# Layer 3's softmax denominators in a four-layer graph network: inverted on 128 nodes at a time instead of once for each feature

## The chip, the cores and the metric

The kernel runs on one core of one Trainium2 chip. The metric is the device time of one execution in microseconds (us); lower is better. The engines are named as in the profile: PE (TensorE), PEld (its weight loads), DVE (VectorE), ACT (ScalarE), POOL (GpSimd) and SP (the queue that issues most DMAs).

## What is computed

Sixteen graphs of 1024 nodes with 128 features pass through four layers. Each layer is a graph layer on the 0/1 matrix adj, a residual and a layer norm. Layer 0 is attention with one head, layer 1 attention with eight heads and an ELU, layer 2 a mean over neighbours with weights, and layer 3, which the change is in, is attention with four heads of 32 features:

```python
def _L3_gnn_ref(features, adj_matrix, W):
    D = W.shape[-1]                                        # 32
    Wh = jnp.einsum('bsf,hfd->bhsd', features, W)          # 4 heads
    scores = jnp.einsum('bhsd,bhtd->bhst', Wh, Wh) / jnp.sqrt(jnp.float32(D))
    scores = jnp.where(adj_matrix[:, None, :, :] > 0, scores, NEG_INF)
    attn = jax.nn.softmax(scores, axis=-1)
    h = jnp.einsum('bhst,bhtd->bhsd', attn, Wh)
    return jnp.transpose(h, (0, 2, 1, 3)).reshape(B, S, H * D)
...
x = _layernorm(x + _L3_gnn_ref(x, adj, L3_gnn_W), axis=-1)
```

The kernel divides by the softmax's denominator (the sum of the exponentials) after the sum over neighbours, once for each node and head.

## The kernel before, in words

Everything below is in `tile_binary`, the function that runs when adj holds only 0 and 1. The second function, `tile_general`, is in the program too, but this input doesn't run it.

**The order of the work.** The functions `before0`, `layer0`, `before1`, `layer1`, `last1`, `layer2`, `before3` and `layer3` issue nothing themselves. They record steps, each with an engine, an assumed duration, a due time and the buffers that it reads and writes. `Plan.run` then walks through all steps once, when the program is built, and writes out a fixed order for every engine: on each engine, of the steps that could start first, it takes the one with the earliest due time. So graph b's layer 1, graph b+1's layer 0 and graph b-1's layer 3 stand interleaved. Due times come from the last lines of the function: graph b is due at b * PERIOD, and each part of it at an offset from that. Some constants shape the order: URGENT makes ACT and DVE steps earlier that touch PSUM, AHEAD limits how far beyond the earliest open due time a step may be taken, LATER1 and LATER3 put off the weighted sums of layers 1 and 3 behind their weights. On the chip each engine keeps its order and waits for its inputs by semaphores. The assumed durations take no part in that.

**Buffers.** Pools have few places. "wk" in PSUM has two of 1024 numbers a partition, and takes all short products; "acc1" and "acc3" have two of 512 each, for layer 1's and layer 3's accumulators. In SBUF, "z" (9 places) holds layer 1's weights, "z3" (5 places) layer 3's, "oT1" (one place, 1024 wide) layer 1's result before it is transposed and the exponentials of its ELU, "oT3" (one place, 512 wide) layer 3's, and "rest" (one place) a piece of layer 2's and layer 3's inverted sums.

**Layer 1** is most of DVE's work: L778 makes each weight tile of 128x1024 in one instruction, and L786 multiplies it into acc1. At the end of a group of heads ACT copies acc1 into oT1 (L816), PE transposes it (L366), and DVE inverts the sums that lie in the transposed tile (L831) and multiplies (L835).

**Layer 2** runs its 192 products a graph in one burst (L918). Ahead of it L886 and L893 on DVE take products out of "wk".

**Layer 3** works on one half of the nodes (512) at a time, with 8 blocks of 128 neighbours in each. For a block, ACT makes the mask (L1066), PE adds the mask (L1076) and the scores (L1086) into two "wk" places, ACT takes exponentials (L1129), and PE adds the weighted features into one acc3 place, "values" (L1098), and the sums of weights into the other, "sums" (L1108). In some blocks DVE first adds the weights of two blocks (L1143), so that their sum is taken once. Both accumulators have features on the partitions, four heads of 32, and the 512 nodes along the free axis. The sums therefore stand there 32 times for each head, one for each feature. At the end of a half DVE inverts all 128x512 sums (L1156) into "rest", multiplies the values by them into "oT3" (L1159), PE transposes the result into "wk" (L366, the helper `transposes`), and DVE adds it to x3 (L1170) and takes row sums (L405) for the layer norm, which runs on ACT (L430, L458), DVE and POOL (L446).

Of the kernel before, what the change touches and what calls it, by code (L numbers as in the profile page):

```python
# [24 lines left out]
ALU = mybir.AluOpType  # L25
# [3 lines left out]
P = 128  # L29
HALF = 512  # L30
# [46 lines left out]
class Plan:  # L77
# [4 lines left out]

    LAG = 0.2
    SLACK = 0.00
    URGENT = 67.5
    SWITCH = 0.1
    SAME = 0.0
    AHEAD = 346.0

    def __init__(self):  # L90
        self.steps = []
# [13 lines left out]
    def step(self, engine, us, due, emit, reads=(), writes=(), lag=None, holds=(), floor=0.0, mode="full"):  # L105
        s = Step(engine, us, due, emit, self.LAG if lag is None else lag, mode)
        s.ready = floor
        for buf in holds:
            s.bufs.append(buf)
            buf.left += 1  # L110
        follows = set()
        for keys, writing in ((reads, False), (writes, True)):
            for key in keys:
                buf, part = key if isinstance(key, tuple) else (key, None)
                if buf not in s.bufs:
                    s.bufs.append(buf)
                    buf.left += 1
                buf.parts.setdefault(part, [None, []])
                for p, (writer, readers) in buf.parts.items():
                    if part is None or p is None or p == part:  # L120
                        if writer:
                            follows.add(writer)
                        if writing:
                            follows.update(readers)
        for keys, writing in ((reads, False), (writes, True)):
            for key in keys:
                buf, part = key if isinstance(key, tuple) else (key, None)
                if writing:
                    for p in list(buf.parts):
                        if part is None or p == part:  # L130
                            buf.parts[p] = [s, []]
                else:
                    buf.parts[part][1].append(s)
        follows.discard(s)
        if engine in ("ACT", "DVE") and any(buf.pool in self.scarce for buf in s.bufs):
            s.due -= self.URGENT
        s.waits = len(follows)
        for f in follows:
            f.next.append(s)
        self.steps.append(s)  # L140
        return s
# [83 lines left out]
def tile_binary(  # L225
# [20 lines left out]
    nc = tc.nc  # L246
    B, N, F = x.shape
    NB = N // P
    HB = NB // 2
    H1, _, D1 = w1.shape  # L250
    H3, _, D3 = w3.shape
# [17 lines left out]
    ident = const.tile([P, P], F32, name="b_ident")  # L269
# [20 lines left out]

    TOGETHER = {(0, 3), (1, 3)}
    LATER1 = 7.4
    LATER3 = 15.9


    sbuf = ctx.enter_context(tc.tile_pool(name="bsbuf", bufs=1))
# [2 lines left out]
    def places(pool, count, shape, dtype=F32):  # L299
        tiles = [sbuf.tile(shape, dtype, name=f"{pool}_{n}") for n in range(count)]  # L300
        plan.pool(pool, tiles)
        return tiles

    def little(pool, shape):
        if pool not in plan.places:
            places(pool, 2, shape)
        return Buf(pool, pool)
# [29 lines left out]
    places("xT0", 2, [P, HALF])  # L337
    places("rest", 1, [P, HB, P])
    places("rT", 1, [H1 * NB, P])
    places("whT", 3, [P, HALF])  # L340
    places("turn", 3, [P, HALF])
    places("gap", 6, [P, HALF], BF16)
# [11 lines left out]
    step = plan.step  # L354
# [5 lines left out]
    def blocks_of(t):  # L360

        return t.rearrange("p (k c) -> p k c", c=P)

    def transposes(pt, parts):
        for k, part in enumerate(parts):
            nc.tensor.transpose(pt[:, k * P : (k + 1) * P], part, ident)  # L366
# [42 lines left out]
    def layernorm(y, tot, due, rest=None, half=None):  # L409


        off, squared, rstd, shift = (little(n, [P, NB]) for n in ("off", "squared", "rstd", "shift"))
        junk = little("junk", [P, P])
        ks = slice(0, NB) if half is None else slice(half * HB, (half + 1) * HB)
        pairs = range(ks.start // 2, ks.stop // 2)
        tot_of = (tot, half)

        def minus_mean():
            if rest:
                nc.vector.scalar_tensor_tensor(  # L420
                    off.t, in0=tot.t, scalar=-1.0 / F, in1=rest.t, op0=ALU.mult, op1=ALU.add
                )
            else:
                nc.vector.tensor_scalar(off.t[:, ks], tot.t[:, ks], -1.0 / F, None, ALU.mult)  # L424

        step("DVE", 0.1, due, minus_mean, [tot_of, rest] if rest else [tot_of], [off])

        def square(pair):
            for k in (2 * pair, 2 * pair + 1):
                nc.scalar.activation(  # L430
                    junk.t, y.t[:, k, :], AF.Square, bias=off.t[:, k : k + 1], accum_out=squared.t[:, k : k + 1]
                )

        for pair in pairs:
            step(
                "ACT", 1.05, due + pair, lambda pair=pair: square(pair), [off, (y, pair // 2)], [(squared, pair), junk]
            )
        due += 4
        step(
            "DVE", 0.1, due,  # L440
            lambda: nc.vector.tensor_scalar(rstd.t[:, ks], squared.t[:, ks], 1.0 / F, EPS, ALU.mult, ALU.add),  # L441
            [squared], [rstd],
        )
        step(
            "POOL", 2.3, due,
            lambda: nc.gpsimd.tensor_tensor(rstd.t[:, ks], rstd.t[:, ks], neg_half[:, ks], ALU.pow),  # L446
            [], [rstd], lag=0.3,
        )
        due += 3
        step(  # L450
            "DVE", 0.1, due,
            lambda: nc.vector.tensor_tensor(shift.t[:, ks], off.t[:, ks], rstd.t[:, ks], ALU.mult),  # L452
            [off, rstd], [shift],
        )

        def apply(pair):
            for k in (2 * pair, 2 * pair + 1):
                nc.scalar.activation(  # L458
                    y.t[:, k, :], y.t[:, k, :], AF.Identity, bias=shift.t[:, k : k + 1], scale=rstd.t[:, k : k + 1]
                )  # L460

        for pair in pairs:
            step("ACT", 0.77, due + pair, lambda pair=pair: apply(pair), [shift, rstd], [(y, pair // 2)])
# [380 lines left out]
    def last1(b, due):  # L844

        G = graphs[b]
        o, x1, e = G["x2"], G["x1"], Buf("oT1", "e")
        step(
            "ACT", 1.0, due, lambda: nc.scalar.activation(e.t, o.t.rearrange("p k f -> p (k f)"), AF.Exp), [o], [e]
        )  # L850
        step(
            "DVE", 1.14, due,
            lambda: nc.vector.scalar_tensor_tensor(o.t, in0=o.t, scalar=0.0, in1=x1.t, op0=ALU.max, op1=ALU.add),
            [x1], [o],
        )
        step(
            "DVE", 1.14, due,
            lambda: nc.vector.scalar_tensor_tensor(o.t, in0=blocks(e.t), scalar=1.0, in1=o.t, op0=ALU.min, op1=ALU.add),
            [e], [o],
        )  # L860
        tot = little("tot", [P, NB])
        for half in range(2):
            sums(o, half, tot, due)
        layernorm(o, tot, due + 3)
# [185 lines left out]
    def layer3(b, due, span):  # L1050
# [1 line left out]
        x3, m, whTs, turns, low, hhs = G["x3"], G["m"], G["whT"], G["turn"], G["low"], G["hh3"]  # L1052
        tot = little("tot", [P, NB])

        def flat(rest):
            return rest.t.rearrange("p k c -> p (k c)")

        for half in range(2):
            cols = slice(half * HALF, (half + 1) * HALF)

# [55 lines left out]
            for j in range(NB):  # L1116
# [33 lines left out]
                else:  # L1150
# [1 line left out]
                        "PE", 0.87, at + LATER3, lambda j=j, zs=zs, f=summed: f(j, zs), zs, [sums3], mode="32 columns"  # L1152
                    )
            at = due + span * (half + 1) / 2
            oT, pt, rest = Buf("oT3", "oT3"), Buf("wk", "pb3"), Buf("rest", "shares")
            step("DVE", 0.6, at, lambda sums3=sums3, rest=rest: nc.vector.reciprocal(flat(rest), sums3.t), [sums3], [rest])  # L1156
            step(
                "DVE", 0.6, at,
                lambda values=values, rest=rest, oT=oT: nc.vector.tensor_tensor(oT.t, values.t, flat(rest), ALU.mult),  # L1159
                [values, rest], [oT],  # L1160
            )
            step(
                "PE", 0.44, at,
                lambda oT=oT, pt=pt: transposes(pt.t, [oT.t[:, k * P : (k + 1) * P] for k in range(HB)]),
                [oT], [pt],
            )
            ks = slice(half * HB, (half + 1) * HB)
            step(
                "DVE", 0.6, at,
                lambda ks=ks, pt=pt: nc.vector.tensor_tensor(  # L1170
                    x3.t[:, ks, :], x3.t[:, ks, :], blocks_of(pt.t[:, :HALF]), ALU.add
                ),
                [pt], [(x3, half)],
            )
            sums(x3, half, tot, at)
            if b == B - 1:
# [12 lines left out]


    PERIOD = 131.4
    weights(-213)
    for b in range(B):
        at = b * PERIOD
        at0 = 71 if b == 1 else at
        before0(b, at0 - 52)
        layer0(b, at0)
        before1(b, at - 70)
        layer1(b, at + 82, 123)
        last1(b, at + 184)  # L1200
        layer2(b, at + 147)
        before3(b, at + 175)
        layer3(b, at + 302, 133)
    with tc.manual_schedule():
        plan.run()
# [626 lines left out]
```

## Time and profile before

| what | value |
|---|---|
| median of three runs | 2421.48 us (2417.6 to 2427.45) |
| the profiled execution's own time | 2421.31 us |
| its span in the profile | 2419.5 us |
| mean granted PE clock | 0.961 |
| busy: PE, DVE, ACT, POOL | 2122.6, 2037.9, 1684.1, 284.4 us |
| layer 3's reciprocal, L1156 | 32 instructions, 107.2 us busy, 3351 ns each |
| layer 3's multiply L1159, and add L1170 | 32 each, 692 and 681 ns each |
| first and last L1156 | 318.2 and 2401.0 us |

How to read the profile: a row names the line, the engine, the operation, the tiles written and read, the shapes and the number of instructions; then come the busy time in us and the mean duration of one in ns, then the idle time of the engine just before these instructions and what ended it. The chain of waits is followed back from the last instruction: at each step to the work that released it, or to the instruction before it on the same engine. A stretch row gives, for a stretch of time, the busy time of each engine in it. fp32 products are two records each in the profile, since PE runs them in two passes.

### The profile page before, as it was taken

The numbers are of one execution on the slowest core, as the hardware profiler recorded it, in microseconds if no ns is written. First come the engines' busy times: TensorE is split into PE (matmuls) and PEld (weight loads), VectorE is DVE, ScalarE is ACT, GpSimd is POOL, SyncE is SP. The second block draws the span as 40 slices with busy tenths as digits, with TensorE's granted clock in tenths as the row PEclk, the third lists the DMA queues.
The fourth block names the chain that finished last, engine by engine and source line by source line (L and its number), as shares of the span: only waits on it lengthen the run. The fifth ranks groups of instructions, "written<-read, shape, count | busy, mean of one in ns | idle before, by whom it ended". The sixth has DMA issues, their size and how long they took to land.

```text
span 2419.5 us, 50524 instructions
## 1 busy us (share of the span) xinstructions
PE 2122.6 (88%) x21040; PEld 991.1 (41%) x21040; DVE 2037.9 (84%) x2659; ACT 1684.1 (70%) x4150; POOL 284.4 (12%) x268
## 2 busy tenths in 40 slices
PE   5758799899999999999999989999999989898876
PEld 5416244353535344353544435353534426242321
DVE  3899789889989898999989898999999979898322
ACT  3314667678586868868686977868686876767684
POOL 2000011101011011101111110101101110100000
PEclk8879899999999999999999999999999999999998
DMA  6211220403122040312204041222204131200000
GB/s 101 68 54 28 82 34 19 88 28 89 28 88 37 10 98 27 91 26 89 36 31 93 11 95 30 85 31 89 36 10 97 27 82 25 71 10 10 1 10 11
DMA packets 80832, 119.55 MB, mean 49 GB/s; under 512 B 7384, under 2 KB 58704, under 8 KB 80592
## 3 DMA queue, kind: packets, MB, share of 16 engines
q1 hardware_dynamic: 62160, 99.43, 12.1%
q0 software_dynamic: 18432, 16.79, 8.5%
q8 instruction: 167, 2.74, 0.5%
q14 instruction: 73, 0.60, 0.1%
HBM read 157.55 MB, written 8.97 MB: 69 GB/s over the span
## 4 chain that ended last, share of the span: by engine, by line
DVE 39%; PE 36%; ACT 17%; issue 5%; DMA 2%; POOL 2%; POOLq 0%; DVEq 0%; ACTq 0%
DVE z L778 24%; PE wk L918 7%; PE acc L786 6%; PE acc L638 6%; ACT z L1129 5%; PE wk L1086 4%; PE acc L1098 4%; DVE rest L1156 4%; PE wk L366 3%; ACT junk L430 3%; PE acc L1108 3%; ACT turn L1003 2%; ACT x L458 2%; DVE z L1143 2%; PE wk L1076 2%
## 5 line engine op out<-in xcount | busy, mean ns | idle before, releaser
L778 DVE SCALAR_TENSOR_TENSOR z<-R,q,m 128x1024 f32<-128x1024 f32 x1024 | 1253.7, 1278 | 18.9 <-PE acc L786 10.2
L1129 ACT ACTIVATE z<-wk,low 128x1024 f32<-128x1024 f32 x512 | 545.6, 1107 | 88.3 <-PE wk L1086 79.6
L786 PE MATMUL acc<-z,hh 128*32 128x512 f32 x4096 | 526.0, 628 | 80.0 <-DVE z L778 75.0
L430 ACT ACTIVATE junk<-x,off 128x128 f32<-128x128 f32 x640 | 257.4, 402 | 317.3 <-DVE off L424 293.6
L446 POOL TENSOR_TENSOR rstd<-rstd,b_neg_half 128x8 f32<-128x8 f32 (+1 forms) x81 | 176.8, 2183 | 1196.9 <-DVE rstd L441 1056.6
L1086 PE MATMUL wk<-whT,turn 32*128 32x512 f32 x2048 | 297.9, 652 | 0.0
L458 ACT ACTIVATE x<-x,shift,rstd 128x128 f32<-128x128 f32 x640 | 261.6, 490 | 46.3 <-DVE shift L452 46.2
L1098 PE MATMUL acc<-z,hh 128*32 128x512 f32 x2048 | 280.0, 616 | 14.1 <-DVE rest L1156 14.1
L1108 PE MATMUL acc<-z,ones 128*32 128x512 f32 x1792 | 261.1, 614 | 28.7 <-DVE z L1143 27.8
L786 PEld LDWEIGHTS acc<-z,hh 128*32 128x32 f32 x4096 | 115.1, 113 | 390.7 <-issue 209.1
L638 PEld LDWEIGHTS acc<-hd,z 128*128 128x128 f32 x2048 | 240.2, 194 | 59.5 <-ACT x L659 19.0
L638 PE MATMUL acc<-hd,z 128*128 128x129 f32 x2048 | 252.9, 280 | 10.4 <-ACT x L659 8.9
L918 PEld LDWEIGHTS <-m 128*128 128x128 fp8e5 x3072 | 179.0, 98 | 16.5 <-issue 16.5
L918 PE MATMUL wk<-y,m 128*128 128x128 bf16 (+1 forms) x3072 | 180.7, 219 | 3.5 <-ACT z L1129 3.5
L1066 ACT ACTIVATE gap<-m,neg_one 128x512 bf16<-128x512 fp8e5 x256 | 183.3, 720 | 0.0
L1076 PE MATMUL wk<-gap,far 32*32 32x512 bf16 x4096 | 133.9, 389 | 50.4 <-ACT z L1129 19.1
L626 DVE SCALAR_TENSOR_TENSOR z<-R,q,m 128x512 f32<-128x512 f32 x240 | 165.1, 745 | 8.9 <-DMA R<-rows 8.9
L1076 PEld LDWEIGHTS <-far 32*32 32x32 bf16 x4096 | 43.0, 88 | 265.2 <-issue 262.9
L1156 DVE RECIPROCAL rest<-acc 128x512 f32<-128x512 f32 x32 | 107.2, 3351 | 39.0 <-PE acc L1108 39.0
L1108 PEld LDWEIGHTS acc<-z,ones 128*32 128x32 f32 x1792 | 50.1, 110 | 184.5 <-issue 120.2
L430 ACT ACTIVATION_READ_ACCUMULATOR junk<-x,off 128x1 f32 x640 | 120.4, 188 | 0.0
L1098 PEld LDWEIGHTS acc<-z,hh 128*32 128x32 f32 x2048 | 48.8, 110 | 150.0 <-issue 123.6
(115 smaller groups left out, 1914.1 us busy)
## 6 DMA issues: line engine op xcount, KB each, us to landing
R<-rows SPq DMA_DIRECT2D x139, 512.0 KB
m<-in_adj_dram POOLq DMA_DIRECT2D x128, 128.0 KB, 4.7
xT<-in_xT_dram SPq DMA_DIRECT2D x32, 256.0 KB
x<-in_x_dram SPq DMA_DIRECT2D x16, 512.0 KB
out_dram<-x SPq DMA_DIRECT2D x15, 512.0 KB
rows<-rT SPq DMA_DIRECT2D x16, 32.0 KB
out_dram<-x SPq DMA_DIRECT2D x2, 256.0 KB
z<-in_L_gnn_a_dram SPq DMA_DIRECT2D x2, 128.0 KB
```

What stands on the lines that cost most here:

```text
L430: nc.scalar.activation(junk.t, y.t[:, k, :], AF.Square, bias=off.t[:, k : k + 1], accum_out=squared.t[:, k : k + 1])
L458: nc.scalar.activation(y.t[:, k, :], y.t[:, k, :], AF.Identity, bias=shift.t[:, k : k + 1], scale=rstd.t[:, k : k + 1])
L638: nc.tensor.matmul(av[k // 2].t.rearrange("p (k c) -> p k c", k=2)[:, k % 2, : P + 1], lhsT=z.t[:, at : at + P], rhs=hd.t[:, j, : P + 1], ...
L778: nc.vector.scalar_tensor_tensor(z.t, in0=G["R"][h].t, scalar=q.t[:, j, h : h + 1], in1=m[j].t, op0=ALU.max, op1=ALU.mult)
L786: nc.tensor.matmul(av[half].t[32 * c : 32 * c + 32, :], lhsT=hh.t[:, j, at : at + 32], rhs=zs[c].t[:, half * HALF : (half + 1) * HALF], st ...
L918: nc.tensor.matmul(ps.t[:, k * SLOT : k * SLOT + part.stop - part.start], lhsT=m[j].t[:, rows_i], rhs=y2.t[:, j, part], start=j == 0 and n ...
L1076: nc.tensor.matmul(sc[h // 2].t[c * 32 : (c + 1) * 32, (h % 2) * HALF : (h % 2 + 1) * HALF], lhsT=far[rows_r, rows_r], rhs=gap.t[rows_r, : ...
L1086: nc.tensor.matmul(sc[h // 2].t[:, (h % 2) * HALF : (h % 2 + 1) * HALF], lhsT=turns[j // HB].t[rows_h, j % HB * P : (j % HB + 1) * P], rhs ...
L1098: nc.tensor.matmul(values.t[rows_h, :], lhsT=hhs[j // HB].t[:, j % HB, rows_h], rhs=zs[h // 2].t[:, h % 2, :], start=j == 0, stop=j == NB - 1,
L1108: nc.tensor.matmul(sums3.t[h * D3 : (h + 1) * D3, :], lhsT=ones, rhs=zs[h // 2].t[:, h % 2, :], start=j == 0, stop=j == NB - 1,)
L1129: lambda g=g, sc=sc, zs=zs: nc.scalar.activation(zs[g].t.rearrange("p h n -> p (h n)"), sc[g].t, AF.Exp, bias=low.t, scale=S3),
L1156: step("DVE", 0.6, at, lambda sums3=sums3, rest=rest: nc.vector.reciprocal(flat(rest), sums3.t), [sums3], [rest])
```

## The change

In layer 3 the values and the sums are now both copied out of PSUM by ACT, into the two halves of one "oT1" place. PE then brings both to a layout with nodes on the partitions: the values by the four transposes as before, and the sums by four products with every 32nd column of the identity, which picks one number of each head. A group of 128 nodes thus gives four columns, and a half gives 16 a partition. DVE inverts these 16, multiplies the transposed values by them with a broadcast over the 32 features, into "rest", and adds the result to x3. "oT3" is left to the squares in `before3`. The layer norm's "junk" has one place in place of two. The planner's constants and the due offsets of most parts have other values.

```diff
-    URGENT = 67.5
+    URGENT = 79.2
...
-    AHEAD = 346.0
+    AHEAD = 411.0
...
-    LATER3 = 15.9
+    LATER3 = 20.9
...
+    places("junk", 1, [P, P])
...
-        junk = little("junk", [P, P])
+        junk = Buf("junk", "junk")
...
-            oT, pt, rest = Buf("oT3", "oT3"), Buf("wk", "pb3"), Buf("rest", "shares")
-            step("DVE", 0.6, at, lambda sums3=sums3, rest=rest: nc.vector.reciprocal(flat(rest), sums3.t), [sums3], [rest])
+            oT, pt, o = Buf("oT1", "oT3"), Buf("wk", "pb3"), Buf("rest", "o3")
+            rd = little("rd3", [P, HB, H3, 1])
+            for n, of in enumerate((values, sums3)):
+                step(
+                    "ACT", 0.48, at,
+                    lambda n=n, of=of, oT=oT: nc.scalar.copy(oT.t[:, n * HALF : (n + 1) * HALF], of.t), [of], [(oT, n)],
+                )
+
+            def natural3(oT=oT, pt=pt):
+
+                for k in range(HB):
+                    at, at0 = HALF + k * H3, HALF + k * P
+                    nc.tensor.matmul(
+                        pt.t[:, at : at + H3], lhsT=oT.t[:, at0 : at0 + P], rhs=ident[:, 0:P:D3],
+                        start=True, stop=True,
+                    )
+                transposes(pt.t, [oT.t[:, k * P : (k + 1) * P] for k in range(HB)])
+
+            step("PE", 0.8, at, natural3, [oT], [pt])
+
+            def share(pt=pt, rd=rd, o=o):
+                nc.vector.reciprocal(
+                    rd.t, pt.t[:, HALF : HALF + HB * H3].rearrange("p (k h u) -> p k h u", k=HB, u=1)
+                )
+                nc.vector.tensor_tensor(
+                    o.t.rearrange("p k (h d) -> p k h d", h=H3),
+                    pt.t[:, :HALF].rearrange("p (k h d) -> p k h d", k=HB, h=H3),
+                    rd.t.to_broadcast([P, HB, H3, D3]),
+                    ALU.mult,
+                )
+
+            step("DVE", 0.8, at, share, [pt], [rd, o])
+            ks = slice(half * HB, (half + 1) * HB)
             step(
                 "DVE", 0.6, at,
-                lambda values=values, rest=rest, oT=oT: nc.vector.tensor_tensor(oT.t, values.t, flat(rest), ALU.mult),
-                [values, rest], [oT],
-            )
-            step(
-                "PE", 0.44, at,
-                lambda oT=oT, pt=pt: transposes(pt.t, [oT.t[:, k * P : (k + 1) * P] for k in range(HB)]),
-                [oT], [pt],
-            )
...
-                lambda ks=ks, pt=pt: nc.vector.tensor_tensor(
-                    x3.t[:, ks, :], x3.t[:, ks, :], blocks_of(pt.t[:, :HALF]), ALU.add
-                ),
-                [pt], [(x3, half)],
+                lambda ks=ks, o=o: nc.vector.tensor_tensor(x3.t[:, ks, :], x3.t[:, ks, :], o.t, ALU.add),
+                [o], [(x3, half)],
             )
...
-    weights(-213)
+    weights(-196)
...
-        before0(b, at0 - 52)
+        before0(b, at0 - 45)
...
-        before1(b, at - 70)
-        layer1(b, at + 82, 123)
-        last1(b, at + 184)
-        layer2(b, at + 147)
-        before3(b, at + 175)
+        before1(b, at - 66)
+        layer1(b, at + 82, 124)
+        last1(b, at + 146)
+        layer2(b, at + 129)
+        before3(b, at + 198)
```

More of the change, by code (lines that the diff above doesn't have):

```diff
@@ L1053, in layer3 @@
         tot = little("tot", [P, NB])
-        def flat(rest):
-            return rest.t.rearrange("p k c -> p (k c)")
         for half in range(2):
@@ L1154, in layer3 @@
             at = due + span * (half + 1) / 2
-            oT, pt, rest = Buf("oT3", "oT3"), Buf("wk", "pb3"), Buf("rest", "shares")
-            step("DVE", 0.6, at, lambda sums3=sums3, rest=rest: nc.vector.reciprocal(flat(rest), sums3.t), [sums3], [rest])
-            step(
-                "DVE", 0.6, at,
-                lambda values=values, rest=rest, oT=oT: nc.vector.tensor_tensor(oT.t, values.t, flat(rest), ALU.mult),
-                [values, rest], [oT],
-            )
-            step(
-                "PE", 0.44, at,
-                lambda oT=oT, pt=pt: transposes(pt.t, [oT.t[:, k * P : (k + 1) * P] for k in range(HB)]),
-                [oT], [pt],
-            )
+            oT, pt, o = Buf("oT1", "oT3"), Buf("wk", "pb3"), Buf("rest", "o3")
[25 more added lines that the diff above has]
+            step("DVE", 0.8, at, share, [pt], [rd, o])
             ks = slice(half * HB, (half + 1) * HB)
```

## The prediction

> **What bounds the kernel now.** I read first the page's busy shares, then the chain of waits, then the busy time by stretch for the steady part, and last what TensorE waits for there.
>
> ```profile
> PE 2122.6 (88%) x21040; PEld 991.1 (41%) x21040; DVE 2037.9 (84%) x2659; ACT 1684.1 (70%) x4150; POOL 284.4 (12%) x268
> DVE 39%; PE 36%; ACT 17%; issue 5%; DMA 2%; POOL 2%; POOLq 0%; DVEq 0%; ACTq 0%
> DVE z L778 24%; PE wk L918 7%; PE acc L786 6%; PE acc L638 6%; ACT z L1129 5%; PE wk L1086 4%; PE acc L1098 4%; DVE rest L1156 4%; PE wk L366 3%; ACT junk L430 3%; PE acc L1108 3%; ACT turn L1003 2%; ACT x L458 2%; DVE z L1143 2%; PE wk L1076 2%
> ```
>
> To be seen: two engines are nearly full and the chain changes between them. "DVE rest L1156" is the reciprocal that the change replaces. Over the whole span its share in the chain is 3.8%, 92 us of 2419.5.
>
> In the steady part one layer-2 burst (L918, 192 products) follows the next every 138 us (757.42 to 1724.08 is 966.7 us for seven graphs). Busy time in eight stretches of 137 us from 674 to 1770 averages PE 127.6, DVE 126.4, ACT 103.7. So PE has 9.4 us without work in each and DVE 10.6. Neither could give 5% alone. One graph cut finer (columns: us; then busy us of PE, PEld, DVE, ACT, POOL; the granted clock; DMA share and GB/s):
>
> ```profile
> 1104.00:1110.00 6.00, 6.00 (x67) 1.70 (x60) 6.00 (x6) 6.00 (x12) 0.00 (x0) 1.00 0.01 3
> 1110.00:1114.00 4.00, 3.56 (x32) 1.73 (x24) 3.97 (x3) 3.34 (x9) 0.00 (x0) 1.00 0.00 0
> 1114.00:1126.00 12.00, 10.03 (x109) 3.67 (x109) 11.93 (x16) 6.38 (x21) 0.40 (x1) 1.00 0.01 2
> ...
> 1158.00:1162.00 4.00, 3.65 (x23) 2.39 (x24) 3.97 (x3) 4.00 (x10) 0.46 (x1) 1.00 0.91 84
> 1162.00:1167.00 5.00, 3.28 (x20) 1.71 (x18) 5.00 (x6) 1.61 (x4) 1.13 (x3) 1.00 0.86 69
> ```
>
> The two reciprocals of this graph run at 1109.71 and 1158.34. Before the first one PE is full. During and after it DVE is full and PE stands: 0.44 + 1.97 us. Around the second one it is 0.35 + 1.72 us. Together 4.5 of PE's 9.4 us follow a reciprocal. TensorE's waits over the same eight graphs name who was late:
>
> ```profile
> PE wk L366 <- DVE rest L886: 15.7, 8, 2.0
> PE wk L366 <- ACT z L1129: 12.6, 30, 0.9
> PE acc L786 <- DVE z L778: 12.0, 20, 0.7
> PE wk L1076 <- DVE x L835: 10.6, 8, 1.7
> PE acc L1108 <- DVE z L1143: 9.1, 11, 1.9
> PE acc L1098 <- DVE rest L1156: 5.0, 8, 0.9
> ```
>
> The first is layer 3's transposes waiting for a "wk" place that L886 frees, which stands behind reciprocal and multiply on DVE: 2.0 us a graph.
>
> **The change part by part.** The rows for its prices (mean ns after the busy time):
>
> ```profile
> L1156 DVE RECIPROCAL rest<-acc 128x512 f32<-128x512 f32 x32 | 107.2, 3351 | 39.0 <-PE acc L1108 39.0
> L831 DVE RECIPROCAL rd<-wk 128x32 f32<-128x32 f32 x32 | 11.3, 353 | 7.7 <-PE wk L366 6.4
> L835 DVE TENSOR_TENSOR x<-wk,rd 128x512 f32<-128x512 f32 x32 | 22.1, 691 | 1.0
> L816 ACT COPY oT<-acc 128x512 f32<-128x512 f32 x64 | 36.0, 594 | 55.0 <-PE acc L786 55.0
> L638 PEld LDWEIGHTS acc<-hd,z 128*128 128x128 f32 x2048 | 240.2, 194 | 59.5 <-ACT x L659 19.0 <-issue 11.8 <-ACT oT L816 11.7
> L786 PEld LDWEIGHTS acc<-z,hh 128*32 128x32 f32 x4096 | 115.1, 113 | 390.7 <-issue 209.1 <-DVE z L778 155.2 <-ACT x L659 12.3
> ```
>
> *DVE.* Removed per half graph: reciprocal 3.35, multiply 0.69, add 0.68, together 4.72 us. Added: a reciprocal of 16 numbers a partition, a multiply by a broadcast, an add. Reciprocals of 2 and 32 numbers take 161 and 353 ns, so 6.4 ns a number, and 16 take 161 + 14 x 6.4 = 0.25 us. The multiply has L835's form, 0.69. The add now reads two SBUF tensors, as L679 does, 0.68. Sum 1.62. DVE loses 3.10 us a half, 6.2 a graph, 99 us over 32 halves.
>
> *ACT.* Two copies of 128x512 out of PSUM, each 0.59 (L816): +1.19 a half, 2.4 a graph, 38 us in all. ACT goes to 106 us of some 134 a graph, so the engine has room. As ACT already mixes copies with exponentials and the trace holds one table load in all, no reload is priced. Behind the copies stand ACT's exponentials (L1129), and the scores wait for these; in the changed kernel's built order of instructions the copies come right behind an exponential in one half and among layer 2's copies in the other. I charge 0.2 us of PE time a half for that and for the new waits below (lower bound 0, upper 1.2, the whole copies).
>
> *PE.* Four products of 128x128 weights by 4 columns a half, 128 in all; fp32 runs each as two passes, since 1024 products in the built order of L638 are 2048 records. So 256 loads and short matmuls. No row has 4 columns. Loads: L638's mean is 194 ns, but a run of 64 such pairs took 7.66 us, 120 ns a pair with 129 columns each, so loads overlap. L786's loads occupy 115.1/4096 = 28 ns for 32 columns, four times that is 112 ns for 128. The Trainium skill (TensorE: Matmul & The Clock Gate, LDWEIGHTS) says that a load's time goes by its columns, about columns / 1.2 in ns, 107 for these, and (Back-to-back issue gap) that few columns do not make a matmul as cheap as they are, as the spacing is set by load and product together. That speaks against this change: four columns pay for a full load. By the rule 256 x 107 = 27 us; by the mean of L638's row, as if nothing overlapped, 256 x 194 = 50 us; by the bf16 pairs of L918 (192 in 11.29 us, 59 ns) 15 us. I take 112 ns, nearest in type and measured as occupancy: 29 us, 1.8 us a graph, bounds 0.9 and 3.1.
>
> *Moved waits.* The sums' accumulator was freed by the reciprocal (L1098 waits for it, 5.0 us over eight graphs), and is now freed by a copy. The products wait for both copies, and behind them on PE's queue waits everything. In the built order, between the last sums product and the four-column products stand two groups of layer-1 products and four transposes in one half (about 2.6 us by their rows: 0.96 + 0.66 + 0.96), and layer-2 products, transposes and layer-1 products in the other (2 x 2.0 + 0.66 + 0.96 = 5.6 us). Copies take 1.2, so they are covered; without the cover it would be 1.2 us a half. The "wk" place is held until DVE's multiply instead of its add, 0.94 us after DVE gets to it. The single "oT1" place is now shared by layer 1, its ELU and layer 3: in the built order PE or DVE has left the place ahead of the work that makes the next user's input, so nothing is charged. One "junk" in place of two: both writers are ACT, in order; free. No DMA, and nothing on SP or POOL, is added.
>
> *Order.* The changed dues and constants reorder little: at every layer-2 burst of the steady part layers 0 and 1 stand where they stood, to a step or two, and layer 3 one block of scores (a sixteenth of a graph) later. After the last layer-1 product 29 blocks are left instead of 30. Worth nothing that I can price.
>
> **The sum.** Per steady graph, in PE's time: the gaps after the two reciprocals go, -4.5. Of the other gaps where DVE is late (L835 1.3, L1143 1.1) half goes as DVE gains room, -1.2. Products +1.8, new waits +0.4. That is -3.5, period 138 to 134.5, on 14 graphs (reciprocals at 318 to 2205): -49 us. What is late next is PE itself: about 129 busy of 134. In the end part, where only layer 3 is left, two reciprocals on the chain (2331.79 and 2367.55, 3.37 each) become one copy: -2.8 each. The last half's path, 6.1 us from reciprocal to row sums (2400.99 to 2407.07), becomes 0.59 + 0.9 + 1.13 + 0.25 + 0.69 + 0.68 = 4.2, and -1.7 with some 0.2 for handing over. ACT is 38 of 41 us busy from 2291 to 2332 there, so copies cost +1.8. End part: -5.5. The start, up to 318, has no reciprocal: 0. Against the profiled execution's own 2421.31 us (span 2419.5 and 1.8 around it; the median of the runs is 2421.48, the same to 0.2): 2421.3 - 54.5 = 2367 us.
>
> **The rivals.** *(A) As summed*, PE becomes the pace: 2367, chance 0.57, own range 2345 to 2392 (products by either bound: -13 or +18; new waits 0 to 1.2 a half).
> *(B) DVE's time comes off nearly whole.* For it: 28 of 32 reciprocals are on the chain, and with room on DVE every later wait shrinks. Against it: PE would need 129 of 132. 6 us a graph: 2421 - 84 - 5 = 2332, chance 0.2.
> *(C) Hidden by PE.* PE has 93% as it is; the products cost 3.1 and new waits for copies and "wk" eat most of the rest: 4.5 - 3.1 - 0.7 = 0.7 a graph, 2421 - 10 - 3 = 2408, chance 0.14. What the gaps after the reciprocals show speaks against it.
> *(D) Slower: PE's queue stands at the four-column products*, because ACT's in-order copies come after exponentials that themselves wait for PE. Place: once each half. Gain without it is 3.9 a graph, so it decides from 2.0 us a half. At 3 us it gives +2.1 a graph, 2421 + 29 = 2450. Against it stands the cover of 2.6 and 5.6 us, chance 0.09.
>
> About 0.5%, 12 us, is what a measurement of this kernel can tell from no change. A and B are all faster by that; C lies across its edge, so faster 0.84, same 0.08, slower 0.08. The range for eight in ten reaches into B and to C: 2326 to 2408.
>
> **What would show it.** Right: DVE busy near 1939 us, ACT 1722, PE about 2150; period near 134.5; PE's gaps after the shares gone and PE leading the chain; the small reciprocal near 0.25 us. Wrong: the four-column pairs far from 112 ns; long waits of PE on the copies or of ACT on "oT1"; a period below 132, which would say that DVE, not PE, set the pace; or a start that differs by more than 5 us, which would be the constants' doing.

## The result and the profile after

The changed kernel takes 2406.05 us (median of 5 runs, 2404.12 to 2410.23), the kernel before 2420.12 us in the same comparison (5 runs, 2417.6 to 2427.45). The ratio is 0.9942, with an interval of 0.9922 to 0.9962. It is faster by 14 us, which is clear of noise; 54 were forecast. Times below are medians. The profiled execution of the changed kernel has 2404.12 us, with a span of 2401.8. In the changed kernel most lines stand one or two away from their old numbers: the layer-1 weights are L779, the shift of a layer norm L453, POOL's power L447, POOL's all-reduce L399.

The page's engine row, and its chain by engine and by line:

```profile
PE 2137.1 (89%) x21296; PEld 1019.5 (42%) x21296; DVE 1942.6 (81%) x2659; ACT 1710.4 (71%) x4214; POOL 284.2 (12%) x268
DVE 40%; PE 25%; ACT 25%; issue 6%; POOL 3%; DMA 1%; POOLq 0%; DVEq 0%; ACTq 0%
DVE z L779 27%; ACT z L1127 6%; PE acc L639 5%; PE wk L1084 4%; ACT junk L431 4%; PE acc L787 4%; ACT x L459 4%; POOL rstd L447 3%; PE acc L1096 3%; ACT gap L1064 2%; ACT turn L1004 2%; PE acc L1106 2%; PE wk L1074 2%; PE wk L367 2%; PE wk L376 2%
```

DVE lost 95.3 us of work, near the 99 forecast. Yet it still leads the chain with 40%, PE's share fell from 36% to 25%, and a new name is in the list: the power on POOL, L447, with the layer norm's L431 and L459 on either side of it. The new instructions' rows:

```profile
L1174 DVE RECIPROCAL rd<-wk 128x16 f32<-128x16 f32 x32 | 8.0, 251 | 31.4 <-PE wk L367 31.4
L1165 PE MATMUL wk<-b_ident,oT 128*128 128x4 f32 x256 | 33.9, 255 | 1.4 <-ACT oT L1158 0.9
L1158 ACT COPY oT<-acc 128x512 f32<-128x512 f32 x64 | 35.4, 579 | 4.5 <-PE acc L1106 3.3 <-PE acc L1096 1.2
```

The reciprocal costs 251 ns, the four-column pairs occupy PE for 33.9 / 256 = 132 ns each, and a copy takes 579 ns.

The steady part didn't become faster. I take its period from the trace as the distance between the first division by degrees (L935, now L936) of one graph and of the next. Its median over nine graphs in the middle is 137.7 us before and 137.5 after. The gain comes from elsewhere: the first two periods together went from 287.1 to 269.7 us and the 13th and 14th from 290.2 to 276.5, while the ten between became 8.8 us longer (one of them, 151.3 us, holds the wait of 9.8 us at L587 below) and the last one 9.2. What holds DVE now, in the stretch from 674 to 1770 us as in the prediction, first before, then after (engine and line, what ended the wait, us in all, times, longest):

```profile
DVE norms L1033 <- ACT oT L1028: 26.4, 16, 2.5
...
DVE shift L452 <- POOL rstd L446: 9.8, 16, 1.6
```

```profile
DVE shift L453 <- POOL rstd L447: 45.7, 19, 3.9
DVE z L1141 <- PE acc L1096: 18.3, 12, 3.7
DVE x L956 <- ACT x L459: 16.6, 8, 3.1
...
DVE r L587 <- POOL all L399: 9.8, 1, 9.8
```

DVE waits for POOL's power 5.7 us a graph instead of 1.2. This is most of the 6.2 us of work that it was relieved of. Its waits in all rose from 9.9 to 16.4 us a graph. TensorE's waits over the same stretch after the change:

```profile
PE acc L787 <- DVE z L779: 26.7, 16, 2.9
PE wk L367 <- ACT z L1127: 17.1, 29, 3.0
PE wk L376 <- DVE x L836: 8.7, 7, 1.2
```

The waits behind the reciprocals are gone (L366 for L886 had 15.7 us, L1098 for L1156 5.0). Instead PE waits for layer-1 weights: 26.7 us, where it had 12.0. The stretch of one graph in which PE stands longest, and what runs in it (columns as in the prediction):

```profile
962.00:974.00 12.00, 8.88 (x89) 2.81 (x85) 8.12 (x12) 7.27 (x16) 2.54 (x2) 1.00 0.43 149
```

```profile
961.55 1.31 POOL L399 PARTITION_ALL_REDUCE all<-top  x1 [13.81 <-DVE top L713]
...
964.25 0.17 DVE L442 TENSOR_SCALAR rstd<-squared 128x8 f32<-128x8 f32 x1
964.32 1.28 DVE L779 SCALAR_TENSOR_TENSOR z<-R,q,m 128x1024 f32<-128x1024 f32 x1
965.52 1.22 DVE L760 TENSOR_TENSOR hh<-hh 128x1024 f32<-128x1024 f32 x1
966.65 1.28 DVE L779 SCALAR_TENSOR_TENSOR z<-R,q,m 128x1024 f32<-128x1024 f32 x1
...
970.06 1.68 POOL L447 TENSOR_TENSOR rstd<-rstd,b_neg_half 128x8 f32<-128x8 f32 x1 [7.20 <-issue]
971.77 0.17 DVE L453 TENSOR_TENSOR shift<-off,rstd 128x8 f32<-128x8 f32 x1 [3.84 <-POOL rstd L447]
...
973.19 1.92 PE L787 MATMUL acc<-z,hh 128*32 128x512 f32 x16 [2.92 <-DVE z L779]
```

Read it from above. POOL ends an all-reduce at 962.86. Its next instruction is the power, whose input DVE has ready at 964.4. But the power starts only at 970.06: POOL is idle for 7.20 us and waits for nothing that the profile shows ("issue"). In the trace a MODIFY_POOL_CONFIG stands at the head of that idle time. I call such idle time, between an all-reduce and a power, POOL's change of program. DVE has only 3.8 us of other work between L442 and L453, so it stands for 3.84 us, and as it keeps its order, the weights behind L453 are late and PE stands 2.92 us. In the kernel before, an all-reduce and a power also alternate (87 changes, 89 after). This layer norm is layer 3's, whose row sums follow the half's end. The same layer norm of one graph before:

```profile
982.69 0.40 POOL L398 PARTITION_ALL_REDUCE all<-top  x1 [15.85 <-DVE top L712]
...
990.91 0.16 DVE L441 TENSOR_SCALAR rstd<-squared 128x8 f32<-128x8 f32 x1
...
991.16 2.65 POOL L446 TENSOR_TENSOR rstd<-rstd,b_neg_half 128x8 f32<-128x8 f32 x1 [8.07 <-DVE rstd L441]
993.84 0.17 DVE L452 TENSOR_TENSOR shift<-off,rstd 128x8 f32<-128x8 f32 x1 [0.39 <-POOL rstd L446]
```

There the all-reduce ended 8.0 us ahead of L441's end, so POOL's idle time was over when the power's input came, and the shift waited 0.39 us, with only 2.4 us of DVE work between. After the change the distance is 1.55 us, in seven of the eight graphs from 674 to 1770 us. Over these eight graphs this layer norm has 29.1 of the 45.7 us of waits at the shift, where it had 3.1; layer 1's, whose distance fell from 10.1 to 3.7 us, has 11.5, where it had none.

### The profile page after: what moved, and what is told of

Same layout as the page of the kernel before. It is cut to its first block, busy times and chain, and to the rows that moved or that the text cites. A ratio compares the mean times of both kernels' runs of the same rounds, so it can differ in the third digit from the quotient of the medians.

```text
span 2401.8 us, 51111 instructions
## 1 busy us (share of the span) xinstructions
PE 2137.1 (89%) x21296; PEld 1019.5 (42%) x21296; DVE 1942.6 (81%) x2659; ACT 1710.4 (71%) x4214; POOL 284.2 (12%) x268
## 4 chain that ended last, share of the span: by engine, by line
DVE 40%; PE 25%; ACT 25%; issue 6%; POOL 3%; DMA 1%; POOLq 0%; DVEq 0%; ACTq 0%
DVE z L779 27%; ACT z L1127 6%; PE acc L639 5%; PE wk L1084 4%; ACT junk L431 4%; PE acc L787 4%; ACT x L459 4%; POOL rstd L447 3%; PE acc L1096 3%; ACT gap L1064 2%; ACT turn L1004 2%; PE acc L1106 2%; PE wk L1074 2%; PE wk L367 2%; PE wk L376 2%
## 5 line engine op out<-in xcount | busy, mean ns | idle before, releaser
L779 DVE SCALAR_TENSOR_TENSOR z<-R,q,m 128x1024 f32<-128x1024 f32 x1024 | 1253.6, 1277 | 10.1 <-PE acc L787 6.4
L431 ACT ACTIVATE junk<-x,off 128x128 f32<-128x128 f32 x640 | 257.3, 402 | 287.1 <-DVE off L425 265.2
L459 ACT ACTIVATE x<-x,shift,rstd 128x128 f32<-128x128 f32 x640 | 263.0, 488 | 70.7 <-DVE shift L453 69.8
L447 POOL TENSOR_TENSOR rstd<-rstd,b_neg_half 128x8 f32<-128x8 f32 (+1 forms) x81 | 159.6, 1970 | 1146.6 <-DVE rstd L442 848.2
L787 PEld LDWEIGHTS acc<-z,hh 128*32 128x32 f32 x4096 | 113.9, 111 | 389.0 <-issue 193.0
L1106 PE MATMUL acc<-z,ones 128*32 128x512 f32 x1792 | 244.1, 604 | 3.5 <-DVE z L1141 3.3
L431 ACT ACTIVATION_READ_ACCUMULATOR junk<-x,off 128x1 f32 x640 | 120.9, 189 | 0.0
L1141 DVE TENSOR_TENSOR z<-z,z 128x1024 f32<-128x1024 f32 x64 | 77.1, 1221 | 41.0 <-PE acc L1096 40.7
L1084 PEld LDWEIGHTS wk<-whT,turn 32*128 32x128 f32 x2048 | 82.8, 189 | 60.9 <-issue 60.9
```

The lines of the kernel that those rows point to most:

```text
L431: nc.scalar.activation(junk.t, y.t[:, k, :], AF.Square, bias=off.t[:, k : k + 1], accum_out=squared.t[:, k : k + 1])
L459: nc.scalar.activation(y.t[:, k, :], y.t[:, k, :], AF.Identity, bias=shift.t[:, k : k + 1], scale=rstd.t[:, k : k + 1])
L779: nc.vector.scalar_tensor_tensor(z.t, in0=G["R"][h].t, scalar=q.t[:, j, h : h + 1], in1=m[j].t, op0=ALU.max, op1=ALU.mult)
L787: nc.tensor.matmul(av[half].t[32 * c : 32 * c + 32, :], lhsT=hh.t[:, j, at : at + 32], rhs=zs[c].t[:, half * HALF : (half + 1) * HALF], st ...
L1084: nc.tensor.matmul(sc[h // 2].t[:, (h % 2) * HALF : (h % 2 + 1) * HALF], lhsT=turns[j // HB].t[rows_h, j % HB * P : (j % HB + 1) * P], rhs ...
L1106: nc.tensor.matmul(sums3.t[h * D3 : (h + 1) * D3, :], lhsT=ones, rhs=zs[h // 2].t[:, h % 2, :], start=j == 0, stop=j == NB - 1,)
```

## The experiments

The main theory, POOL: what DVE was relieved of is given back where it waits for POOL's change of program. The rivals: PE is the pace anyhow; the new due offsets are bad by themselves; the added copies or products cost more than charged. The variants with an unchanged order have the same instructions in the same order on PE, DVE and ACT as the kernel that they are made from, but for the operation named.

**DVE's time alone** (from the kernel before):

```diff
-nc.vector.reciprocal(flat(rest), sums3.t)
+nc.vector.tensor_scalar(flat(rest), sums3.t, 0.0, 1e-20, ALU.mult, ALU.add)
```

> The kernel before, each engine's order unchanged; L1156's reciprocal of 128x512 is replaced by a multiply-add of the same tiles (0.69 us by DVE's rows instead of 3.35), so the softmax isn't normalised. DVE loses 2.66 us a half, 85 us in all, and nothing is added on PE or ACT. Theory of the prediction (PE's 4.5 us of gaps behind the two reciprocals of a graph go): period 138 to 133.5, 2421 - 63 - 6 = about 2352. Theory POOL (the time saved on DVE is given back where DVE stands at the shift of a layer norm for POOL, which needs some 7 us to change from an all-reduce to the power): part of the gain stays, 2370 to 2400, and the shift's waits for POOL grow from 1.3 us a graph to 3 or more. Theory PE (PE is the pace at 137 us whatever DVE does): 2410 or more.

Measured: 2339.9 us, ratio 0.9674 (0.9657 to 0.969), so 80 us less. The period is 131.4 us.

```profile
PE 2100.3 (90%) x21040; PEld 993.4 (43%) x21040; DVE 1952.8 (84%) x2659; ACT 1683.7 (72%) x4150; POOL 278.8 (12%) x268
PE 39%; DVE 33%; ACT 19%; issue 5%; DMA 2%; POOL 2%; POOLq 0%; DVEq 0%; SPq 0%; ACTq 0%
```

```profile
DVE shift L452 <- POOL rstd L446: 9.4, 18, 1.6
```

Nearly all of the 85 us of DVE work comes off the time. The theory PE is dead. The prediction's theory had 2352, 12 us too slow. The waits for POOL don't grow here, against what the theory POOL expected of this run. So it isn't that the reciprocals covered POOL's change; the order of the kernel before leaves room for it, with or without them (the distance from the all-reduce to layer 3's L441 stays 8.0 us). The changed kernel's order doesn't.

**POOL's change of program taken away** (from the changed kernel, and from the one before):

```diff
-nc.gpsimd.partition_all_reduce(got.t, v.t, P, op)
+nc.gpsimd.tensor_tensor(got.t, v.t, ones[:, : shape[1]], ALU.mult)
```

> The changed kernel, the order of PE, DVE and ACT unchanged; POOL's maximum over partitions (partition_all_reduce) is replaced by a multiply by one on POOL, so the maximum over partitions is left out and POOL never changes between two programs. Theory POOL: the shift's waits for POOL fall from 5.8 us a graph to under 2, the single stretch of 152 us goes, the period falls from 137.2 to about 133: 2406 - 55 - 14 = about 2340, and not above 2365. Theory PE: the period stays at 136 to 137, only the single stall goes: 2390 to 2400. Theory dues (the order itself is bad, through waits other than POOL's): 2385 or more, with the shift's waits gone but others in their place.

> The kernel before, the order of PE, DVE and ACT unchanged, with POOL's maximum over partitions replaced by a multiply by one as in e2: the maximum over partitions is left out. Theory POOL: before the change POOL's program changes were mostly covered by DVE work, the reciprocals among it, so little is won: 1.3 us a graph of shift waits and a single stall of 11.7 us, 2420 - 12 to 30 = 2390 to 2408; the gap to e2 then is near the 54 us that the prediction gave the change. If POOL's change of program is no part of the explanation, before and after win the same and the gap between e5 and e2 stays at 14 us.

Measured: the changed kernel 2334.4 us, ratio 0.9649 (0.9633 to 0.9665); the one before 2386.8 us, ratio 0.9868 (0.9852 to 0.9885). The changed kernel wins 72 us and the other 33. Without POOL's change of program the gap between them is 52 us instead of 14. In e2 DVE's wait at the shift has shrunk to 0.4 us, and PE leads the chain, as the prediction had it for the changed kernel:

```profile
PE 54%; ACT 25%; DVE 17%; issue 3%; POOL 1%; DMA 0%; POOLq 0%; DVEq 0%
```

```profile
PE wk L367 <- ACT z L1127: 10.9, 26, 1.0
...
PE acc L787 <- DVE z L779: 5.5, 10, 1.3
```

The trace of e2 holds two MODIFY_POOL_CONFIG at L447, that of the changed kernel 92. PE's wait for layer-1 weights fell from 26.7 to 5.5 us. So 39 us of the forecast 54 were lost to POOL's change of program. These runs take away the all-reduce's own time too (0.4 to 1.3 us each), so the 72 and 33 are those of both. PE's busy time is 12 and 10 us less in them (granted clock 0.972 and 0.965, where it was 0.965 and 0.961); that is the same in both, so the 39 us between them aren't PE's clock.

**The dues.** The changed structure with the old constants and offsets, and the old structure with the new ones (the diff's lines for constants and offsets, undone or done alone):

> The changed kernel with the planner's constants and due offsets of the kernel before. Theory dues (the new values placed the layer norms badly and cost the gain): 2355 to 2380, the shift's waits for POOL near 1.3 us a graph as before. Theory POOL (any order that the planner writes without knowing the change of program runs into it once the reciprocal is gone): 2390 to 2420, the shift's waits above 3 us a graph. Theory PE: 2400 to 2415.

> The kernel before with the changed kernel's constants and due offsets, and its own reciprocals. If the new offsets are what made room for the waits for POOL, it has shift waits of 4 us a graph or more and is slower than before, 2440 to 2480. If they suit the old structure as well, it lies within 10 us of 2420. Theory POOL expects waits for POOL of 3 us a graph or more only if the order brings a shift within 7 us behind an all-reduce; with 3.35 us of reciprocal still there fewer than in the changed kernel.

Measured: 2455.0 us (ratio 1.0143, 1.0126 to 1.016) and 2461.0 us (1.0175, 1.0154 to 1.0195). All three theories of e3 missed: half of the change is slower than none, either way. In e3 it is POOL again, now also in the other direction, from the power to layer 0's maximum (L587):

```profile
DVE r L587 <- POOL all L399: 64.3, 6, 11.5
DVE shift L453 <- POOL rstd L447: 39.0, 21, 4.3
```

In e6 it is less so: its wait at the shift is 8.9 us in the same stretch, and one wait at layer 0's maximum is 11.1. Among its longest waits are those of DVE for layer 2's burst, 26.9 us where the kernel before has 11.7, and of PE's transposes for the oT tile (L1159), 17.1. The two runs also tell what moved layer 3's layer norm towards the all-reduce: the distance is 8.0 us in e6, as in the kernel before, and 1.55 us in most graphs of e3, as in the changed one. So it goes with the structure, not with the dues.

> The changed structure with the dues of before, POOL's maximum over partitions left out (e3 without the change of program). If the dues mattered only through POOL, it comes to within 15 us of e2, 2325 to 2350. If they matter by themselves, it stays above 2370.

Measured: 2366.3 us (0.9777, 0.9747 to 0.9807). Without POOL's change of program e3 comes down by 89 us, but it stays 32 us above e2. The old dues cost 49 us with POOL's change of program (e3 less the changed kernel) and 32 without it, so they matter mostly by themselves and for some 17 us through POOL. The limits that I had set for the two answers, 2350 and 2370, leave it between them.

**The prices of copies and products,** each made twice, in the changed kernel and in e2:

```diff
-nc.scalar.copy(oT.t[:, n * HALF : (n + 1) * HALF], of.t)
+[nc.scalar.copy(oT.t[:, n * HALF : (n + 1) * HALF], of.t) for _ in range(2)]
...
+                for k in range(HB):
+                    at, at0 = HALF + (HB + k) * H3, HALF + k * P
+                    nc.tensor.matmul(pt.t[:, at : at + H3], lhsT=oT.t[:, at0 : at0 + P], rhs=ident[:, 0:P:D3], start=True, stop=True)
```

> The changed kernel with each of layer 3's two copies out of PSUM made twice over the same place, otherwise the same order. It prices the added ACT work: 38 us more of ACT. The prediction charged 0.2 us of PE time a half for copies and new waits, 6 us over the kernel: the time should grow by 0 to 12. If ACT's copies are what ate the gain, it grows by 25 us or more.

> e2 (2334 us: changed kernel, no maximum over partitions, POOL with one program) with layer 3's two copies made twice. Theory POOL-amplified (the 29 us of e8 came from queues that POOL had already made late): +0 to +12. If the copies cost ACT's time in full whatever POOL does: +25 to +38.

> The changed kernel with each of the four-column products made twice, into unused columns of the same wk place. It prices one set in place. The prediction's term was 112 ns a pair, 29 us of PE over the kernel: if that is right, PE's busy time grows by 29 us and the time by 15 to 29. By PE's busy time so far (2122.6 before, 2137.1 after) it is nearer 57 ns a pair: busy time +15, time +5 to +15. If PE isn't the pace anywhere, 0.

> e2 with the four-column products made twice. PE is the pace in e2 (54% of its chain), so the products should cost their occupancy, 132 ns a pair by the changed kernel's rows, 34 us in all, on the steady part at least: +25 to +34. If they hide in PE's waits: under +10.

Measured: copies twice 2435.1 us in the changed kernel (+29) and 2358.3 in e2 (+24); products twice 2436.6 (+31) and 2358.7 (+24). The products come out close to the forecasts (15 to 29 in the changed kernel, 25 to 34 in e2). The copies don't: their second set takes 36 us of ACT and costs 24 to 29 us of time, not 0 to 12. Where it is paid, e2 first, then e2 with copies twice:

```profile
L1165 PE MATMUL wk<-b_ident,oT 128*128 128x4 f32 x256 | 33.0, 252 | 0.7 <-ACT oT L1158 0.7
L1165 PE MATMUL wk<-b_ident,oT 128*128 128x4 f32 x256 | 33.4, 254 | 15.2 <-ACT z L1127 8.0 <-ACT oT L1158 7.2
```

PE stands 15.2 us ahead of the four-column products, for the copies and for exponentials behind them. With one set it stands 0.7 us there, 1.4 in the changed kernel. So the first set was nearly covered at this place, and the second wasn't: the price of the second is no measurement of the first, and is likely too high for it.

**Do the parts add?** From e1, with POOL's maximum replaced as well:

> The order of the kernel before, the reciprocal replaced by a multiply-add (no normalisation), and POOL's maximum over partitions by a multiply by one (no maximum). If DVE's saving (80 us in e1) and POOL's change of program (33 us in e5) add: 2421 - 80 - 33 = 2308. If the same waits are behind both, 2320 to 2340. The difference from e2 (2334) is then what products, copies and the other dues cost together: 26 us if they add, none if not.

Measured: 2304.6 us (0.9517, 0.9485 to 0.9549). The gain of 114 us beside its own runs of the kernel before is the sum of 80 and 33, so DVE's time and POOL's change are two costs and not one. From here to e2 it is 30 us up: products, copies and the other order, less 10 us more of DVE's work saved.

**A cure.** The planner is told that POOL needs 7.4 us when it goes from one program to the other; the work is the same.

```diff
+    CHANGE = 7.4
...
             t, s = best
+            if s.mode in ("all", "pow"):
+                if pooled not in (None, s.mode):
+                    t = max(t, left_pool + self.CHANGE)
+                pooled = s.mode
...
             end = now[s.engine] = t + s.us
+            if s.mode in ("all", "pow"):
+                left_pool = end
```

> The changed kernel, the same work; only the planner is told that POOL needs 7.4 us between an all-reduce and a power, either way round, so it places the shifts and what waits for the maxima later in DVE's order. Theory POOL: DVE's waits for POOL fall from 7.0 us a graph (5.7 at the shift, 1.2 at layer 0's maximum) to under 2, the time comes to 2335 to 2370. Theory dues (no order written with these due offsets is good): above 2390.

> The kernel before with its own dues, only the planner is told of POOL's 7.4 us. If the cure helps whatever the structure, it gains about what leaving out the change of program gave it, 33 us: 2385 to 2400. If POOL's change of program hurts the changed kernel in the main, it gains less than 15 us, or loses by the order's other effects.

> The changed structure with the dues of before (2455 us) and the planner told of POOL's 7.4 us. Theory POOL: its waits for POOL (6.7 us a graph for layer 0's maximum, 4.8 at the shift) go for the most part and it falls by 50 to 90 us, to 2365 to 2405. If the dues as such make it slow, it stays above 2430.

> As f1 (2373 us), with 9.0 us told in place of 7.4. f1 still has 3.2 us a graph of waits at the shift, as the power itself takes up to 2.7 us and the change up to 8. More room should take these waits under 2 us a graph and give 2355 to 2373; if the waits go and the time does not, PE and the other waits hold it at 2370 to 2385.

Measured: f1, on the changed kernel, 2373.1 us (0.9806, 0.979 to 0.9823). It is faster than both kernels, 33 us below the changed one, if just above the 2370 expected. f4, on the kernel before, 2383.8 (0.9844, 0.982 to 0.9868). f2, with the old dues, 2394.8 (0.9881, 0.986 to 0.9903), 60 us below e3. With the cure in both, the change is thus worth some 11 us (f4 less f1), not 52. f6 missed: 2419.2 (0.9988, 0.9972 to 1.0003), its periods alternate between about 132 and 146 us, though the shift is no longer among its longest waits. In f1 some of the wait at the shift is left:

```profile
DVE shift L461 <- POOL rstd L455: 25.2, 20, 3.1
```

So three of the four orders that the planner wrote with this knowledge are faster by 33 to 60 us, with no work left out. The fourth, f6, has the shortest waits at the shift (4.2 us) and wins nothing: how much a new order wins or loses beside these waits is luck to some tens of us, and the gains of the other three can't be put to POOL alone.

**The maximum without POOL** (from the changed kernel): a transpose by PE, a row maximum and a multiply with the identity by DVE, a product with ones by PE, a copy by DVE.

> The changed kernel with the maxima over partitions made by PE and DVE (a transpose, a row maximum, a product that spreads it to all partitions) in place of POOL's all-reduce, so POOL keeps one program. It costs 48 times two small products, three small DVE instructions, and a wk place for some 2 us. Theory POOL: no waits of DVE for POOL above 1 us a graph, 2340 to 2370, at most 20 above the 2334 of the run that left the maximum out. If the wk place matters more, PE's waits on wk grow and it stays above 2380.

Measured: 2413.6 us (0.9966, 0.9951 to 0.9981). That is far from the 2340 to 2370 of the theory POOL. The waits for POOL fell to 1.5 us a graph, not quite under 1, and the time didn't follow: PE is busier by 2 us a graph, it waits 2.9 us a graph for "wk" at the mask products (1.1 in the changed kernel), and the period is 138.8 us.

## Why the prediction was wrong

The direction, DVE's saving and most of the sum hold; the time is 39 us off. The step that failed is "What is late next is PE itself": DVE's waits for POOL's change of program came next, and the runs without that change put 39 us on them.

- *DVE's work.* -99 us forecast, -95.3 measured; the small reciprocal 0.25, measured 0.251. Right.
- *What this is worth.* The sum's gaps of 4.5 and 1.2 us a graph on 14 graphs are 80 us, and 5.5 at the end. e1, in which nothing else is changed, wins 80 us, with the period down by 6.3. Right in size. The mechanism holds in the main: PE's waits for L886 (15.7 us over eight graphs), L1156 (5.0) and L1170 (4.8) are gone from its list in e1, and those for the layer-1 weights fell from 12.0 to 3.6, together 4.2 us a graph. But 80 of 85 us is also what rival B said, DVE's time coming off nearly whole; e1 doesn't part the two.
- *Products.* 112 ns a pair forecast, 132 measured; 25 us of time forecast on the steady part, 24 and 31 in all for a second set. Right in size. The mean of the load's row, 195 ns, would have been wrong as a price and the rule's 107 somewhat low.
- *Copies.* Charged, with the new waits, 0.4 us a graph, 6 us in all. The first set's cover held: PE stands 1.4 us in all ahead of the four-column products. "So the engine has room" doesn't follow from ACT's 106 us of 134, though: a second set, with ACT at 1742.6 us busy of 2358.2, costs 24 to 29 us. What the first set costs through the work behind it on ACT isn't measured by itself.
- *What is late next.* This is the step that failed. DVE's waits for POOL were late next, and PE's waits for layer-1 weights behind them (26.7 us, 5.5 without POOL's change). The sum said that nothing is added on POOL, which is true, and left out that DVE's waits for POOL's results move with the order. The rows were in the trace of before, where the second has gaps of 7.8 us on average:

```profile
DVE shift L452 <- POOL rstd L446: 55.3, 33, 11.7
POOL rstd L446 <- issue: 85.4, 11, 10.4
```

- *Order.* "Worth nothing that I can price" failed. I compared where layers stand at each layer-2 burst, which hardly moved. What moved is the all-reduce ahead of a layer norm's L442: it ends 1.55 us before layer 3's, where it ended 8.0 us before it. The first two periods are 17 us shorter, and a start that differs by more than 5 us was one of the signs of being wrong. It isn't the constants' doing alone: these periods are 280.8 us with the old dues (e3) and 291.3 with the new dues alone (e6), where before and after have 287.1 and 269.7.
- *The end.* The last half's path from accumulator to row sums was 6.1 us and should become 4.2; the chain shows 2385.63 to 2389.66, 4.0. Right. From the last graph's first division by degrees to the end of the span it is 145.1 us, 147.8 before: 2.7 us won there, where 5.5 were forecast for the end part.
- *Rivals.* Forecast C gave 2408, close to the time, but for another reason (PE full). e1 and e2 refute that reason, so its number is right by luck.

The account: without POOL's change of program the change is worth 52 us (e5 less e2). DVE's time is 80 of it by e1, or some 90 if the 95.3 us count at the rate of e1's 85.1 (an estimate). The products cost 24 (g3). That leaves 14 us for the copies, the other order and the rest, which aren't measured apart; the forecast had 6 for the copies and new waits. POOL's change of program takes back 39 of the 52, so 13 are left, and 14 were measured.

## What to carry to other kernels

When an engine is relieved and its order is written anew, look for its instructions that wait for a slow engine. Count the work between the request and the wait, and look at what the slow engine did just before the request: here an all-reduce moved from 8.0 to 1.55 us ahead of a power's input, and the change of program behind it became a wait. An order written from assumed durations should know such costs, which depend on what the engine did before. Free time on an in-order engine is no room by itself: PE stood 1.4 us ahead of its products for one set of copies, and 15.2 us for two (in e2's form).

## What the hardware showed

POOL needs 6.6 to 8.3 us from the end of an all-reduce to the start of a power whose input is ready (7.20 us in the place shown), every time that the two alternate, not only the first time. In the other direction, from a power to layer 0's all-reduce, it is 9.2 to 10.3 us in the kernel before and 10.9 at the one such place of the changed kernel, where DVE waits 9.8 us. The Trainium skill (GPSIMD Engine Reference, Instruction dispatch) gives approximately 6 µs for loading a kernel's code at its first call, with no instruction of its own in the profile. Here it is longer. A MODIFY_POOL_CONFIG row marks its start, within 0.3 us of the end of the instruction before it. So it is hidden when the next instruction's input comes later than that: the power at 991.16 us of the kernel before, whose input came 8.0 us after the all-reduce, starts 0.1 us behind its input.
